# PSUM as three shared pairs of banks, and four tiles of scores in a row, in a graph attention kernel of 32 batches

## The chip, the cores and the metric

The kernel runs on one core of one Trainium2 chip. The metric is the device time of one execution in microseconds (us); the figure for a kernel is the median of its runs.

## What is computed

Two layers over 32 batches of 512 nodes with 512 features, all in float32. The first is masked attention with 8 heads of 64, the second a graph convolution; each is added to its input and normalized.

```python
# layer 0
q, k, v = (x @ Wq + bq), (x @ Wk + bk), (x @ Wv + bv)      # per head: 512 x 64
scores = einsum('bihd,bjhd->bhij', q, k) / sqrt(64) + where(adj == 0, -1e9, 0)
out = einsum('bhij,bjhd->bihd', softmax(scores), v)
x = layernorm(x + out)
# layer 1
deg_inv_sqrt = where(adj.sum(1) > 0, rsqrt(adj.sum(1)), 0)
norm_adj = adj * deg_inv_sqrt[:, None] * deg_inv_sqrt[None, :]
x = layernorm(x + norm_adj @ (x @ weight) + bias)
```

## The kernel before

**Steps.** The work is a list of 128 steps, `blocks`: one for each batch and each pair of heads (`ORDER`, four pairs). The loop over `k` (line 819) writes one step after another in program order; a wrapper, `InOrder`, keeps every engine in exactly this order, and every instruction therefore carries the wrapper's line, L44, in the profile. So groups are told apart by tile names.

**One step.** The scores of a step are four tiles, each 128 keys by two heads by 512 queries, two banks of PSUM each. `scores((b, g, jj))` makes two of them: TensorE writes `sc`, VectorE takes it out with the clip and the mask (`e<-sc,maskT`), ScalarE makes the exponential in place. `values` multiplies the exponentials of the step before with V into the one bank `av` (16 matmul instructions), and VectorE turns that bank (`yb<-av`). `accumulate` adds the four `e` tiles on GpSimd, one (`acc<-e`) and then two (`acc<-acc,e`) instructions, the last two put off through `pending` and `put_off`. `fold` turns and reduces that sum on VectorE one step later (`acc<-acc`, `folded<-acc`). In program order a step is: two tiles of scores, fold, values, two more tiles of scores, and then its share of other work.

**Shares.** The other work is what prepares the next batch and finishes the batch before. Each product with weights is done in a form with seven products of half size (`seven`, and `second` for the convolution); one product fills one bank (`mm`) with 8 matmul instructions and is then taken out by VectorE, at times by ScalarE. `cut` deals the products of a batch over its four steps. In the steady part (batches 2 to 30) the four kinds of step are called here:
- step a (line 821, `at == 1`): the seven products of V (`values_of`) and the first of K and Q, with the tail of the convolution's layer norm (`rest`: statistics, root, stores), the inverse of the softmax sums (`inverse_all`), `scale` (VectorE, `yT<-yT,inv`) and `add` (GpSimd, `yT<-yT,xr`);
- step b: the next eight products of K and Q (`keys_and_queries`), with the attention's layer norm: `measure` (VectorE), `root` (GpSimd, `rstd` and `add`), `norm` (ScalarE, `yT<-yT,add,rstd` and `hi<-yT,dis`), `low` (VectorE, `lo<-yT,dis,hi`), `lift` (GpSimd, `yT<-yT,b_r`);
- step c: products of K and Q, and the first half of the convolution (`first`, four products of twice the length in time, taken out by ScalarE);
- step d: the last product of K and Q and the seven of `second`, with the first two `measure` of the convolution's layer norm.

The dictionary `beside` (line 849) says behind which product each small piece stands. On GpSimd, in step a, the sum `u<-u,bv_r` stands between the fourth and the fifth product of V: VectorE waits for it.

**PSUM.** Eight banks: `ps_mm` has three single banks for products, `ps_sc` two pairs for scores, `ps_av` one bank.

The `e` tiles have six buffers: the third and fourth tile of a step are written over the first two of the step before, which `values` of this step reads.

Of the kernel before, what the change touches and what calls it, by code (L numbers as in the profile page):

```python
# [9 lines left out]
F32 = mybir.dt.float32  # L10
# [7 lines left out]
P = 128  # L18
H = 8
# [30 lines left out]
def unshifted(  # L50
# [37 lines left out]
    acts = ctx.enter_context(tc.tile_pool(name="acts", bufs=2))  # L88
    work = ctx.enter_context(tc.tile_pool(name="work", bufs=2))
    small = ctx.enter_context(tc.tile_pool(name="small", bufs=3))  # L90
    ps_mm = ctx.enter_context(tc.tile_pool(name="ps_mm", bufs=3, space=bass.MemoryType.PSUM))
    ps_sc = ctx.enter_context(tc.tile_pool(name="ps_sc", bufs=2, space=bass.MemoryType.PSUM))
    ps_av = ctx.enter_context(tc.tile_pool(name="ps_av", bufs=1, space=bass.MemoryType.PSUM))

# [28 lines left out]

    def turn_first(j, i):

        p = ps_mm.tile([P, 2, HALF], F32, name="mm")
        for n in range(2):
            for u in range(2):  # L130
                for q in range(4):
                    at = q * P + (2 * i + u) * 32
                    tensor.matmul(
                        p[32 * q : 32 * (q + 1), u, ts(n, P)], R[0][2 * j + n][:, at : at + 32], ident,
                        start=True, stop=True,
                    )
        (scalar.copy if i else vector.tensor_copy)(XT[:, 2 * j + i], p)
# [103 lines left out]
    def adjacency(m):  # L241


        p = ps_mm.tile([P, N], F32, name="mm")
        for n in range(NT):
            tensor.transpose(p[:, ts(n, P)], adj_sb[:, n, ts(m, P)], ident)
        vector.tensor_scalar(maskT[:, m, :], p, 0.0, FAR, op0=ALU.is_equal, op1=ALU.mult)
        scalar.copy(adjT[:, m, :], p)
        scalar.copy(plainT[:, m, :], p)
# [36 lines left out]
    def seven(multiply, first, middle, out):  # L286

        t = {}

        def piece(k, i, j):  # L290
            p = ps_mm.tile([P, 2, HALF], F32, name="mm")
            multiply(p, i, j)
            if k == 0:
                t["e1"] = work.tile([P, 2, HALF], F32, name="e1", bufs=1)
                first(t["e1"], p)
            elif k == 1:
                vector.tensor_add(out(0, 0), t["e1"], p)
            elif k == 2:
                t["u1"] = t["e1"]
                vector.tensor_add(t["u1"], t["e1"], p)  # L300
            elif k == 3:
                t["u2"] = work.tile([P, 2, HALF], F32, name="u2", bufs=1)
                middle(t["u2"], t["u1"], p)
            elif k == 4:
                vector.tensor_add(out(1, 1), t["u2"], p)
                vector.tensor_add(t["u1"], t["u1"], p)
            elif k == 5:
                vector.tensor_sub(out(1, 0), t["u2"], p)
            elif k == 6:
                vector.tensor_add(out(0, 1), t["u1"], p)  # L310

        order = [(0, 0), (1, 1), (5, 5), (6, 6), (4, 4), (3, 2), (2, 3)]
        return [(2.1, piece, (k, *args)) for k, args in enumerate(order)]
# [59 lines left out]
    def scores(s):  # L373

        b, g, jj = s
        E[s] = [work.tile([P, 2, N], F32, name="e", bufs=6) for _ in range(2)]
        for l in range(2):
            j = 2 * jj + l
            e = E[s][l]
            p = ps_sc.tile([P, 2, N], F32, name="sc")  # L380
            for k in range(2):
                r = slice(k * HD, (k + 1) * HD)
                tensor.matmul(p[:, k, :], KQ[b, g][r, 0, ts(j, P)], KQ[b, g][r, 1, :], start=True, stop=True)
            vector.scalar_tensor_tensor(
                e, p, CUT, maskT[:, j, None, :].to_broadcast([P, 2, N]), op0=ALU.min, op1=ALU.subtract
            )
            scalar.activation(e, e, AF.Exp)
# [20 lines left out]
    def values(s):  # L408

        b, g, jj = s  # L410
        e = E.pop(s)
        if jj == 0:
            AV[b, g] = ps_av.tile([P, N], F32, name="av")
        av = AV[b, g]
        for l in range(2):
            j = 2 * jj + l
            for k in range(2):
                tensor.matmul(
                    av[k * HD : (k + 1) * HD, :], V[b][:, j, ts(2 * g + k, HD)], e[l][:, k, :],
                    start=j == 0, stop=j == NT - 1,  # L420
                )
        if jj == 0:
            return
        if (b, g) == blocks[-1]:
            turned = work.tile([P, N], F32, name="avT", tag="yb", bufs=1)
            scalar.copy(turned[:, :HALF], av[:, :HALF])
            vector.tensor_copy(turned[:, HALF:], av[:, HALF:])
            AV[b, g] = turned
            return

        yb = work.tile([P, 4, NT, 32], F32, name="yb", bufs=1)
        vector.transpose(
            yb.rearrange("p l i s -> p i l s"), av.rearrange("p (i r l) -> p i l r", i=NT, l=4)
        )
        if g == ORDER[0]:
            if b < B - 1:
                YT[b] = acts.tile([P, NT, D], F32, name="yT")
            else:  # L440
                YT[b] = wv[:, :NT].rearrange("p k u o -> p k (u o)")
        for q in range(4):
            nc.sync.dma_start(
                YT[b][:, :, (4 * g + q) * 32 : (4 * g + q + 1) * 32],
                yb[32 * q : 32 * (q + 1)],
            )
# [13 lines left out]
    def sums(b, c):  # L460


        p = ps_mm.tile([P, N], F32, name="mm")
        for q in range(4):
            parts = ACC[b, ORDER[2 * c + q // 2]]
            for k, a in enumerate(parts):
# [31 lines left out]
    def finish(b):  # L498
# [3 lines left out]

        def inverse_all():

            p = ps_mm.tile([P, H, NT, 4], F32, name="mm")
            tensor.matmul(
                p.rearrange("p h i l -> p (h i l)"), spread.rearrange("p q r -> p (q r)"),
                SM[b].rearrange("p h t -> p (h t)"), start=True, stop=True,
# [8 lines left out]

        def inverse(cs):
            sT = SM[b]
            p = ps_mm.tile([P, NT, 2, 2, 32], F32, name="mm")  # L520
            for i in range(NT):
                tensor.transpose(p[:, i].rearrange("p a k r -> p (a k r)"), sT[:, ts(i, P)], ident)
            if cs[0] == 0:
# [22 lines left out]

        def turn_values(g):

            t["y"] = ps_mm.tile([P, NT, P], F32, name="mm")
            for i in range(NT):  # L550
                tensor.transpose(t["y"][:, i], AV[b, g][:, ts(i, P)], ident)

# [9 lines left out]
                )  # L562

        def measure(i):
            if i == 0:
                t["mv"] = small.tile([P, NT, 2], F32, name="mv")
            statistics(YT[b][:, i, :], t["mv"][:, i, :])

# [35 lines left out]
        def block(f):  # L604
            return [(0, f, (i,)) for i in range(NT)]

        return dict(
            early=[(0.6, inverse, ((0,),))], late=[(0.6, inverse, ((1,),)), (0.6, turn_values, (ORDER[-1],))],
            pairs=[[(0, add_pair, (i, g)) for i in range(NT)] for g in ORDER],
            halves=[(0, root, (0, 2)), (0, root, (2, 2))],  # L610
            inverse=[(0.6, inverse_all, ())], scale=block(scale), add=block(add), measure=block(measure), root=[(0, root, ())],
            judge=[(0, judge, ())], norm=block(norm), low=block(low), lift=block(lift), grow=block(grow),
        )

    def weave(side, main):
# [8 lines left out]
    def convolve(b):  # L624
# [3 lines left out]
        last = b == B - 1  # L628

        def first(d):  # L630
            p = ps_mm.tile([P, N], F32, name="mm")
            for m in range(NT):
                tensor.matmul(p, HI[b][:, m, ts(d, P)], adjT[:, m, :], start=m == 0, stop=False)
                tensor.matmul(p, LO[b][m][:, ts(d, P)], adjT[:, m, :], start=False, stop=m == NT - 1)
# [1 line left out]

        def block(m):
            if m == 0:
                t["p"] = [ps_sc.tile([P, 2, N], F32, name="sc") for _ in range(2)]
            for part, start, stop in ((HI[b][:, m, :], m == 0, False), (LO[b][m], False, m == NT - 1)):  # L640
                for d in range(DT):
                    p = t["p"][d // 2][:, d % 2]
# [23 lines left out]
            return tile[:, 2 * j : 2 * j + 2, ts(i, HALF)]  # L666

        def second(k, i, j):
            p = ps_mm.tile([P, 2, HALF], F32, name="mm")
            for r in range(2):  # L670
                for u in range(2):
                    tensor.matmul(
# [146 lines left out]
    for k in range(S + 1):  # L819
        b, at = divmod(k, G)  # L820
        if at == 1:
# [22 lines left out]
            elif b < B - 1:  # L844
# [2 lines left out]


                beside = {
                    0: rest[:1], 1: rest[1:3], 3: rest[3:4] + put_off, 4: rest[4:5],  # L850
                    5: rest[5:6] + f["inverse"] + put_off, 6: rest[6:] + f["scale"][:2], 7: f["scale"][2:] + f["add"],
                    8: measure[:2] + put_off, 9: measure[2:], 10: f["root"] + put_off, 11: norm[:1],
                    12: norm[1:2] + low[:1], 13: norm[2:3] + low[1:2], 14: norm[3:] + low[2:3],
                    15: low[3:] + f["lift"], 16: put_off + grow[:2], 17: put_off + grow[2:], 18: turn0 + f["judge"],
                }
                side = sum(([piece] + beside.get(i, []) for i, piece in enumerate(main)), [])
                side += c["first"] + c["parts"] + kq[5:] + turn1[:1]
# [33 lines left out]
            run(early[:2])  # L891
        if k and blocks[k - 1][0] < B - 1:
            fold(*blocks[k - 1])
        if k:
            values((*blocks[k - 1], 0))
            if k == S:
# [3 lines left out]
                sums(blocks[k - 1][0], (k - 1) % G // 2)  # L900
        if k == S - 2:
            run(within)
            scores((*blocks[k], 1))
            pending += [((*blocks[k], jj),) for jj in range(2)]
        elif k < S:
            accumulate((*blocks[k], 0))
            scores((*blocks[k], 1))
            if b == B - 1:
                accumulate((*blocks[k], 1))
            else:  # L910
# [29 lines left out]
    run(e["unload"] + e["parts"] + s[6:] + end["grow"] + extend[2:] + c["measure"][:2])  # L940
    s, tail, halves = e["second"], c["measure"][2:] + c["root"] + c["store"], e["halves"]
    run(s[:2] + halves[0] + s[2:3] + tail[:1] + s[3:4] + tail[1:3] + s[4:5])
    p = ps_mm.tile([1, 1], F32, name="mm")
    tensor.matmul(p, count, ones, start=True, stop=True)
    vector.tensor_scalar(bad, p, -1.0, float(P * B * NT * H + N), op0=ALU.mult, op1=ALU.add)
    run(tail[3:] + s[6:] + e["measure"][2:] + e["roots"][1:] + e["stores"][2:] + s[5:6] + halves[1] + e["roots"][:1])
# [284 lines left out]
```

## Time and profile before

| | |
|---|---|
| median of 3 runs | 2856.01 us (2855.47 to 2856.58) |
| the profiled execution, its own time | 2858.47 us |
| its span, first to last instruction | 2856.4 us |
| granted TensorE clock | 0.997 |
| TensorE weight loads, busy | 1865.2 us (65%) |
| VectorE, busy | 2301.6 us (81%) |
| GpSimd, busy | 1846.0 us (65%) |
| ScalarE, busy | 1046.8 us (37%) |
| DMA, mean | 49 GB/s |
| one batch in the steady part | 87.79 us (1312.35 to 1400.14) |

All times within the span are counted from its start. In the timeline a row reads: start, duration, engine, line, operation, out<-in, shapes, number of equal instructions that follow each other, and in brackets the idle time before it and what ended it. A float32 matmul of the program is two matmul instructions on the engine. "mean ns" of an instruction is its own latency; instructions of one engine overlap at their ends, so what a row costs is read from the start of the next.

### The profile page before, as it was taken

To read this page: it belongs to the slowest core of one execution; us is meant where nothing else is said; L and a number is where in the kernel's file an instruction comes from. 1 tells how busy PE (TensorE), PEld (TensorE's weight loads), DVE (VectorE), ACT (ScalarE), POOL (GpSimd) and SP (SyncE) were. 2 spreads that over 40 slices of the span, in tenths; PEclk is the share of its full clock that TensorE was granted. 3 is DMA by queue.
4 is the path that set the end of the run, shared out by engine and by line. 5 is a ranking of instruction groups with operands and counts; after the bars stand their busy time and mean duration, and the time that the engine had idled before them with its cause. 6 is when DMAs were issued, how large, how long until landed. Compare 5 with 4: busy or idle time off the path is not lost.

```text
span 2856.4 us, 34678 instructions
## 1 busy us (share of the span) xinstructions
PE 2817.5 (99%) x12540; PEld 1865.2 (65%) x12540; DVE 2301.6 (81%) x3201; ACT 1046.8 (37%) x1323; POOL 1846.0 (65%) x1174
## 2 busy tenths in 40 slices
PE   8999999999999999999999999999999999999997
PEld 6566666666666666666666666666666666666655
DVE  5878877888778887788887788877888778788787
ACT  2333333343333433333333334333343333333344
POOL 3666666766666666666666676666666666666666
PEclk9999999999999999999999999999999999999999
DMA  4111122111221112221112211122112222111211
GB/s 118 32 29 48 49 56 46 41 47 49 59 56 42 37 48 56 56 45 41 49 48 58 51 41 41 50 58 56 41 37 51 53 56 45 41 49 48 59 38 50
DMA packets 379108, 141.05 MB, mean 49 GB/s; under 512 B 277808, under 2 KB 345392, under 8 KB 378928
## 3 DMA queue, kind: packets, MB, share of 16 engines
q1 hardware_dynamic: 377776, 137.17, 20.1%
q8 instruction: 101, 1.65, 0.2%
q10 hardware_dynamic: 1152, 1.57, 0.2%
q14 instruction: 79, 0.65, 0.1%
HBM read 71.83 MB, written 33.55 MB: 37 GB/s over the span
## 4 chain that ended last, share of the span: by engine, by line
PE 78%; DVE 19%; issue 2%; POOL 0%; DMA 0%; ACT 0%; DVEq 0%; POOLq 0%; ACTq 0%
PE mm L44 52%; PE sc L44 13%; PE av L44 12%; DVE yT L44 5%; DVE e L44 5%; DVE st L44 3%; DVE acc L44 1%; DVE u L44 1%; DVE mv L44 1%; DVE yb L44 1%; DVE v L44 1%; DVE kq L44 1%; DVE xT L44 0%; DVE plainT L44 0%; POOL xT L44 0%
## 5 line engine op out<-in xcount | busy, mean ns | idle before, releaser
L44 ACT ACTIVATE e<-e 128x1024 f32<-128x1024 f32 x512 | 540.8, 1057 | 1166.2 <-DVE e L44 1137.2
L44 POOL TENSOR_TENSOR acc<-acc,e 128x1024 f32<-128x1024 f32 x248 | 588.9, 2375 | 188.3 <-ACT e L44 181.0
L44 DVE SCALAR_TENSOR_TENSOR e<-sc,maskT 128x1024 f32<-128x1024 f32 x512 | 597.5, 1207 | 22.1 <-PE sc L44 21.9
L44 PE MATMUL sc<-kq 64*128 64x512 f32 x2048 | 523.2, 623 | 3.5 <-DVE e L44 3.3
L44 PE MATMUL mm<-xT,wk 128*128 128x256 f32 x1792 | 476.3, 388 | 13.7 <-DVE u L44 11.3
L44 PE MATMUL av<-e,v 128*64 128x512 f32 x2048 | 467.9, 598 | 0.0
L44 PE MATMUL mm<-xT,wq 128*128 128x256 f32 x1792 | 460.7, 380 | 0.0
L44 POOL TENSOR_TENSOR acc<-e 128x1024 f32<-128x1024 f32 x126 | 297.2, 2358 | 230.4 <-ACT e L44 230.4
L44 PEld LDWEIGHTS mm<-xT,wk 128*128 128x128 f32 x1792 | 327.8, 190 | 143.1 <-issue 73.1
L44 PE MATMUL mm<-wv,xT 128*128 128x256 f32 x1792 | 404.3, 383 | 1.7 <-DVE xT L44 1.1
L44 PEld LDWEIGHTS mm<-wv,xT 128*128 128x128 f32 x1792 | 335.6, 190 | 72.3 <-issue 25.4
L44 PEld LDWEIGHTS mm<-xT,wq 128*128 128x128 f32 x1792 | 341.1, 190 | 46.5
L44 PEld LDWEIGHTS sc<-kq 64*128 64x128 f32 x2048 | 171.3, 186 | 290.7 <-issue 150.9
L44 PEld LDWEIGHTS av<-e,v 128*64 128x64 f32 x2048 | 135.5, 136 | 316.2 <-issue 293.4
L44 PE MATMUL mm<-w,zT 128*128 128x256 f32 x992 | 224.9, 379 | 0.7 <-ACT side L44 0.7
L44 POOL TENSOR_TENSOR rstd<-ve,minus_half 128x4 f32<-128x4 f32 (+1 forms) x66 | 66.2, 1003 | 232.5 <-DVE nmu L44 232.5
L44 DVE TENSOR_TENSOR kq<-u,mm 128x512 f32<-128x512 f32 x128 | 87.8, 686 | 156.5 <-PE mm L44 153.0
L44 POOL TENSOR_TENSOR yT<-yT,b_r 128x512 f32<-128x512 f32 x124 | 171.2, 1392 | 63.3 <-DVE lo L44 63.3
L44 PEld LDWEIGHTS mm<-w,zT 128*128 128x128 f32 x992 | 188.2, 190 | 28.1 <-issue 1.5
L44 POOL TENSOR_TENSOR yT<-yT,xr 128x512 f32<-128x512 f32 x124 | 192.8, 1584 | 18.8 <-DVE yT L44 18.8
L44 PE MATMUL mm<-adjT,hi 128*128 128x512 f32 x496 | 202.0, 407 | 0.0
L44 PE MATMUL mm<-adjT,lo 128*128 128x512 f32 x496 | 196.0, 395 | 0.9 <-DVE lo L44 0.9
(141 smaller groups left out, 3382.8 us busy)
## 6 DMA issues: line engine op xcount, KB each, us to landing
out_dram<-y SPq DMA_DIRECT2D x127, 256.0 KB, 2.1
x<-in_x_dram SPq DMA_DIRECT2D x248, 128.0 KB, 2.9
yT<-yb SPq DMA_DIRECT2D x496, 64.0 KB, 2.5
xr<-in_x_dram SPq DMA_DIRECT2D x122, 256.0 KB, 3.3
wk<-in_L_gnn_Wk_dram SPq DMA_DIRECT2D x8, 128.0 KB, 5.0
wq<-in_L_gnn_Wq_dram SPq DMA_DIRECT2D x8, 128.0 KB, 4.3
yT<-in_adj_dram SPq DMA_DIRECT2D x1, 1024.0 KB, 6.4
w<-in_L_gnn_weight_dram SPq DMA_DIRECT2D x2, 512.0 KB, 8.1
```

Of the source, the lines that this page charges most:

```text
L44: return self.tc.keep_in_program_order(op(*args, **kwargs))
```

## The change

Four things are edited in `unshifted`; the program has the same arithmetic, in another order.

1. One pool `psum` with three pairs of banks (`WIDE`), one single bank (`narrow`) and one for `av`. Scores always take pairs. A product takes what is next in the order pair, pair, pair, single (it uses one bank of a pair); the count starts anew in each step behind the scores.
2. Both calls of `scores` stand together, ahead of `values`. `fold` stands between them.
3. In `beside`, `root` of the attention's layer norm stands one product earlier and `norm` with it, `inverse` one product earlier and `scale` with it; the put-off sums of GpSimd stand behind the first two products of step a (before: behind the fourth and sixth).
4. `behind` puts block 3 ahead of blocks 0, 1, 2 in `add`, `measure`, `lift` and `grow`. `add` and `lift` are GpSimd's. Since `scale` and `low` on VectorE go in the order 0 to 3, GpSimd now begins when VectorE has done the last block; before, it began when VectorE had done the first.

```diff
-    ps_mm = ctx.enter_context(tc.tile_pool(name="ps_mm", bufs=3, space=bass.MemoryType.PSUM))
-    ps_sc = ctx.enter_context(tc.tile_pool(name="ps_sc", bufs=2, space=bass.MemoryType.PSUM))
-    ps_av = ctx.enter_context(tc.tile_pool(name="ps_av", bufs=1, space=bass.MemoryType.PSUM))
+    psum = ctx.enter_context(tc.tile_pool(name="psum", bufs=1, space=bass.MemoryType.PSUM))
+    WIDE = dict(tag="wide", bufs=3)
+    turn_of = {"n": 0, "order": (WIDE, WIDE, WIDE, dict(tag="narrow"))}
+
+    def bank(shape, tags=None):
+        if tags is None:
+            order = turn_of["order"]
+            tags = order[turn_of["n"] % len(order)]
+            turn_of["n"] += 1
+        return psum.tile(shape, F32, name="mm", **tags)
...
-            p = ps_sc.tile([P, 2, N], F32, name="sc")
+            p = psum.tile([P, 2, N], F32, name="sc", **WIDE)
...
+        def behind(f):
+            return [(0, f, (i,)) for i in (NT - 1, *range(NT - 1))]
...
-            inverse=[(0.6, inverse_all, ())], scale=block(scale), add=block(add), measure=block(measure), root=[(0, root, ())],
-            judge=[(0, judge, ())], norm=block(norm), low=block(low), lift=block(lift), grow=block(grow),
+            inverse=[(0.6, inverse_all, ())], scale=block(scale), add=behind(add),
+            measure=block(measure) if b == B - 1 else behind(measure), root=[(0, root, ())],
+            judge=[(0, judge, ())], norm=block(norm), low=block(low),
+            lift=block(lift) if b == B - 1 else behind(lift), grow=block(grow) if b == B - 1 else behind(grow),
...
-                    0: rest[:1], 1: rest[1:3], 3: rest[3:4] + put_off, 4: rest[4:5],
-                    5: rest[5:6] + f["inverse"] + put_off, 6: rest[6:] + f["scale"][:2], 7: f["scale"][2:] + f["add"],
-                    8: measure[:2] + put_off, 9: measure[2:], 10: f["root"] + put_off, 11: norm[:1],
-                    12: norm[1:2] + low[:1], 13: norm[2:3] + low[1:2], 14: norm[3:] + low[2:3],
-                    15: low[3:] + f["lift"], 16: put_off + grow[:2], 17: put_off + grow[2:], 18: turn0 + f["judge"],
+                    0: rest[:1] + put_off, 1: rest[1:3] + put_off, 3: rest[3:4], 4: rest[4:5] + f["inverse"],
+                    5: rest[5:6] + f["scale"][:2], 6: rest[6:] + f["scale"][2:] + f["add"],
+                    8: measure[:2] + put_off, 9: measure[2:] + f["root"] + put_off, 10: norm[:1], 11: norm[1:2],
+                    12: norm[2:3] + low[:1], 13: norm[3:] + low[1:2], 14: low[2:3], 15: low[3:] + f["lift"],
+                    16: put_off, 17: put_off + grow[:2], 18: grow[2:] + turn0 + f["judge"],
...
+        if k < S:
+            scores((*blocks[k], 1))
+        else:
+            turn_of["order"] = WIDE, dict(tag="narrow"), dict(tag="av")
+        turn_of["n"] = 0
         if k:
             values((*blocks[k - 1], 0))
...
         elif k < S:
             accumulate((*blocks[k], 0))
-            scores((*blocks[k], 1))
```

Every other `ps_mm.tile(...)` becomes `bank(...)`; `inverse_all` always takes the single bank, and the convolution's `block` of the last batch takes pairs.

## The prediction

> **What bounds the kernel now.** First the page, part 1:
>
> ```profile
> PE 2817.5 (99%) x12540; PEld 1865.2 (65%) x12540; DVE 2301.6 (81%) x3201; ACT 1046.8 (37%) x1323; POOL 1846.0 (65%) x1174
> ```
>
> TensorE is busy all through, and the wait list gives it only one repeated wait (below, 0.38 us in each batch). So the time is TensorE's own order of work plus small losses, and a batch repeats every 87.79 us. I therefore read where TensorE loses time without showing as idle. The timeline of TensorE alone, in one step d:
>
> ```profile
> 1341.96 3.65 PE L44 MATMUL av<-e,v 128*64 128x512 f32 x16
> 1345.55 1.99 PE L44 MATMUL sc<-kq 64*128 64x512 f32 x8
> 1347.47 1.13 PE L44 MATMUL mm<-xT,wk 128*128 128x256 f32 x4
> ...
> 1346.08 1.45 PE L44 MATMUL sc<-kq 64*128 64x512 f32 x6
> ...
> 1346.51 1.02 PE L44 MATMUL sc<-kq 64*128 64x512 f32 x4
> ```
>
> The last two rows are the same run of scores, entered later by a narrower window: its pairs of matmuls start at 1345.55, 1346.08, 1346.51, and the product follows at 1347.47. So pairs are 0.53, 0.43, 0.43, 0.53 apart: a run pays 0.10 on entering and 0.10 on leaving. Values take 3.59 with theirs.
>
> Next, how late VectorE takes up the first tile of a step (the lag D, from the start of the scores), TensorE's rows and then VectorE's, for steps c, a, b:
>
> ```profile
> 1317.72 1.99 PE L44 MATMUL sc<-kq 64*128 64x512 f32 x8
> 1323.30 2.26 PE L44 MATMUL sc<-kq 64*128 64x512 f32 x8
> ...
> 1361.48 1.99 PE L44 MATMUL sc<-kq 64*128 64x512 f32 x8
> ...
> 1383.24 1.99 PE L44 MATMUL sc<-kq 64*128 64x512 f32 x8
> ...
> 1400.14 1.13 PE L44 MATMUL mm<-xT,wk 128*128 128x256 f32 x4 [0.38 <-DVE u L44]
> ```
> ```profile
> 1322.03 2.34 DVE L44 SCALAR_TENSOR_TENSOR e<-sc,maskT 128x1024 f32<-128x1024 f32 x2
> ...
> 1363.61 2.32 DVE L44 SCALAR_TENSOR_TENSOR e<-sc,maskT 128x1024 f32<-128x1024 f32 x2
> ...
> 1382.22 5.18 DVE L44 TENSOR_TENSOR yT<-yT,inv 128x512 f32<-128x512 f32 x4
> 1387.33 2.34 DVE L44 SCALAR_TENSOR_TENSOR e<-sc,maskT 128x1024 f32<-128x1024 f32 x2
> ```
>
> D is 4.31 in c, 2.13 in a, 4.09 in b; in d it is 1.18, no lag (1341.22 against 1340.05). It costs almost nothing now, because between the first tile and the third, which takes the first one's banks, TensorE has 5.5 us of other work. In c the third tile does wait: it starts at 1323.30, 1.27 after VectorE began the first. This 1.27 is what a freed pair costs.
>
> [...] scores use 64 rows, values 64 columns, products the whole array, and each border shows about 0.10 twice. [...] four beside GpSimd's `yT<-yT,xr` took 5.18; two with GpSimd idle took 1.29 (0.60 apart):
>
> ```profile
> 2759.13 1.29 DVE L44 TENSOR_TENSOR yT<-yT,inv 128x512 f32<-128x512 f32 x2
> ```
>
> [...] That is the 0.38 wait: with three banks the fourth product in a row waits for `u`.
>
> **The change, part by part**, in one steady batch; times from the start of a step's scores.
>
> *Four tiles in a row.* One run of scores less per step: 0.20 (its two extras), so 4 x 0.20 = 0.80 gone. The first matmul behind the values pays on entering as it does now behind scores.
>
> *Four banks for products.* The wait for `u` goes: 0.54 (from 1399.60, where the product was due, to 1400.14), 0.10 for entering again, 0.08 of a smaller one before it: 0.72 in step b. In c the waits of the third and fourth tile (0.33), in b one of 0.10, go with the old order.
>
> *Three pairs for four tiles.* New: the fourth tile takes the first tile's pair. It is due at 0.10 + 6 x 0.43 = 2.68 and may start at D + 1.27; so a lag above 1.41 is paid in full, with 0.10 for entering again. Behind it stand values and all products of the step. Products then start 4.64 behind the fourth tile (0.96 for it, 0.09, 3.59), or at 7.22 without a wait; before, at 7.42.
>
> *Lag in a.* VectorE ends d with two sums of the last product, ready only when scores begin, and one statistics pair; nothing of this is edited. D stays 2.13: fourth tile at 3.40, products at 8.04.
>
> *Lag in b.* GpSimd's order in a becomes sum, sum, `rstd`, `add`, sum, `u<-u,bv_r`; before, `u` came ahead of the put-off sums. First product out at 10.07, two statistics, the second at 11.80, `ve` at 13.2; `rstd` and `add` 1.5 (1374.20 to 1375.74), so 14.7; sum 2.36, 17.05; `u` 1.27, 18.3. It would be done at 17.3 without that sum: 1.0 late. VectorE waits for it, then: two V instructions 1.2, inverse 1.25, one 0.6, two `scale`, one 0.6, two `scale`. By `behind`, GpSimd has nothing to do meanwhile, so four `scale` cost 2.4 and not 5.1. Sum 18.3 + 6.05 = 24.4. The step is 8.04 + 14.34 (1368.90 to 1383.24) = 22.38 long. D = 2.1 with a semaphore delay or two; fourth tile at 3.37, products at 8.01.
>
> *Lag in c.* In b: product out at 10.04, four statistics of 0.81 and two products of 0.60, 14.5; `rstd` and `add` to 16.0; ScalarE four times `norm` (0.84 + 0.63), 21.9; its two halves of `e<-mm,bias` stand behind these, 22.7; VectorE `kq` 0.6, last `low` 0.65 without GpSimd beside it, 24.0. Step b is 8.01 + 14.73 - 0.72 = 22.02. D = 1.95; fourth tile at 3.22, products at 7.86.
>
> *Lag in d.* Behind the convolution VectorE has one product: D = 1.18, no wait.
>
> Sum of the batch: a 22.38; b 22.02; c 7.86 + 14.57 = 22.43; d 7.22 + 14.01 = 21.23: 88.06, against 87.79. So +0.27 for each batch: 1.95 is saved, and three waits of 0.82, 0.79 and 0.64 take its place. Over 30 batches +8.
>
> *Both ends.* In the first batch nothing ahead of the lag is edited: by the same rule its D of 4.36, 2.13, 1.88 and, at 127.27, 7.59 cost 2.5, 0.6, 0.4 and 1.1, less 0.2 in one step: +4. At the end of the last batch D is 6.26 in one step (its products are few), worth about 4; behind it TensorE has waits of 1.07, 0.89 and 2.36 on slower chains, which take up part: bounds 0 to +4, I take +2.
>
> *Hidden edits.* The DMAs are the same in kind and number, SP's order too; DMA's mean is 49 GB/s. `lift` and `grow` come later by 2 to 3 us but are needed only in the next step (`lift` ends near 7 of c, `grow` near 13, the convolution's second half is a step away). Without that cover each late us would stand in d.
>
> Total: 2856.4 + 8 + 4 + 2 = 2870 of span. The profiled execution took 2858.5 with a span of 2856.4, the median of the runs is 2856.0; so I add 14 to the median: 2870.
>
> **Rivals.**
>
> Lag gone (faster): GpSimd's sum gets ahead of `rstd`, or ScalarE's chain is shorter than I add up, so that D in b and c falls under 1.41. Then b is 21.23 and c 21.79: 86.63 for a batch, -1.16, -35 in 30; with +4 at the ends 2825. For it: only 0.7 and 0.5 us decide. Against: each step of both chains has a measured row. It decides from D = 1.41 down, 0.1 of lag being worth 3 us in all per step kind.
>
> No relief (slower by much): GpSimd's blocks still meet VectorE's `scale` and `low`, because GpSimd ends step a late. Then D in b grows by 2.7, in c by up to 0.8: +3.5 x 30 = 105, 2975. Against: `add` waits for the last `scale` in the changed program's own waits.
>
> No difference: entering again after a wait costs nothing in a row of scores, -0.3 x 30 = -9 and the ends absorb theirs: 2858. Against: the third tile in c pays it today (1323.30 to the product at 1325.48 is 2.18, not 1.92).
>
> **How the numbers follow.** Likeliest 0.57, at 2870, its own range 2860 to 2884 (each D right to 0.2, so 6 us for each of two steps, and 0 to +4 at the end). Lag gone 0.22; no difference 0.13; no relief 0.08. A measurement of this kernel tells 0.2% (5.7 us) from no change. Slower 0.57 + 0.08 = 0.65, same 0.13, faster 0.22. The range reaches to 2832, inside the first rival, and to 2886; what is left out is the far part of it and the last.
>
> **What would show it.** Right: runs of 16 score matmuls with 3.6 for values behind them; a wait of the fourth tile on `e` of 0.6 to 0.8 in a, b, c and none in d; no wait on `u`; four `scale` in about 2.5 us. Wrong: fourth tiles without waits in b and c, a product that waits for a pair, or `scale` still at 1.3 each. It is wrong in its root if a batch does not take 88.0 to 88.2 us.

## The result, and the profile after

The changed kernel takes 2884.39 us (median of 4 runs, 2883.42 to 2884.67), the kernel before on the same chip 2856.3 us (2855.47 to 2857.94). The ratio is 1.0097, interval [1.0084, 1.0109]: slower by 28 us, where 14 were predicted. The profiled execution took 2884.41 us with a span of 2882.4, granted clock 0.996.

Where the time went is read from TensorE's timeline: the start of the first score matmul of a step cuts the span. Steps are numbered by the loop's `k`; the steady part is k = 6 to 123, 29.5 batches.

| part of the span | before | after | difference | predicted |
|---|---|---|---|---|
| up to the first scores | 55.24 | 51.95 | -3.3 | left out |
| k = 0 to 5 | 98.80 | 106.68 | +7.9 | +4 |
| k = 6 to 123 | 2590.79 | 2606.49 | +15.7 | +8 |
| k = 124 to 126 | 48.25 | 53.10 | +4.9 | +2, with the next row |
| k = 127 and the tail | 63.3 | 64.2 | +0.9 | |
| span | 2856.4 | 2882.4 | +26.0 | +14 |

The other 2 us of the 28 lie outside: before's profiled execution was 2.2 above the median of its runs, after's was not. The means of the steps a, b, c, d (b from k = 10 on: in after the first, k = 6, has a D of 1.25 and no wait):

| | a | b | c | d | batch |
|---|---|---|---|---|---|
| D before | 2.13 | 4.10 | 4.30 | 1.18 | |
| D after | 2.13 | 1.99 | 2.19 | 1.18 | |
| start of the fourth tile, after | 3.38 | 3.26 | 3.47 | 2.68 | |
| length before | 21.75 | 22.30 | 22.32 | 21.43 | 87.80 |
| length after | 22.55 | 21.91 | 22.67 | 21.23 | 88.37 |

TensorE's timeline of after, from the last products of a step d into the scores of a step c (in brackets the idle time before a row and what ended it):

```profile
1460.84 2.85 PE L44 MATMUL sc<-kq 64*128 64x512 f32 x12
1464.22 1.13 PE L44 MATMUL sc<-kq 64*128 64x512 f32 x4 [0.53 <-DVE e L44]
1465.28 3.65 PE L44 MATMUL av<-e,v 128*64 128x512 f32 x16
...
1477.82 3.62 PE L44 MATMUL mm<-wv,xT 128*128 128x256 f32 x16
1481.49 1.10 PE L44 MATMUL mm<-xT,wk 128*128 128x256 f32 x4
...
1483.39 2.85 PE L44 MATMUL sc<-kq 64*128 64x512 f32 x12
1486.65 1.13 PE L44 MATMUL sc<-kq 64*128 64x512 f32 x4 [0.42 <-DVE e L44]
...
1505.31 2.85 PE L44 MATMUL sc<-kq 64*128 64x512 f32 x12
1508.77 1.13 PE L44 MATMUL sc<-kq 64*128 64x512 f32 x4 [0.62 <-DVE e L44]
```

Three tiles run together, and the fourth waits for VectorE to take up the first: 0.53, 0.42 and 0.62 of idle time in a, b and c. From one start to the next the delay is larger, since the fourth tile is due 2.68 after the step's start: 0.70, 0.58, 0.78. The row that follows a wait is 0.10 longer from its start to the next (1464.22 to 1465.28 is 1.06; two pairs of score matmuls and a border are 0.96).

The same stretch on VectorE:

```profile
1462.97 2.32 DVE L44 SCALAR_TENSOR_TENSOR e<-sc,maskT 128x1024 f32<-128x1024 f32 x2
...
1476.07 0.69 DVE L44 TENSOR_TENSOR u<-e,mm 128x512 f32<-128x512 f32 x1 [1.04 <-PE mm L44]
1479.28 0.69 DVE L44 TENSOR_TENSOR v<-u,mm 128x512 f32<-128x512 f32 x1 [2.52 <-POOL u L44]
...
1480.48 0.87 DVE L44 TENSOR_SCALAR inv<-mm 32x32 f32<-32x32 f32 x4
...
1482.37 1.29 DVE L44 TENSOR_TENSOR yT<-yT,inv 128x512 f32<-128x512 f32 x2
...
1484.17 1.29 DVE L44 TENSOR_TENSOR yT<-yT,inv 128x512 f32<-128x512 f32 x2
1485.38 2.35 DVE L44 SCALAR_TENSOR_TENSOR e<-sc,maskT 128x1024 f32<-128x1024 f32 x2
```

The four `scale` (`yT<-yT,inv`) are at 1.29 for two, no longer 5.18 for four. Ahead of them VectorE stands 2.52 us for `u`. GpSimd shows why: its put-off sum stands ahead of `u`.

```profile
1475.50 0.20 POOL L44 TENSOR_TENSOR add<-nmu,rstd 128x4 f32<-128x4 f32 x1
1475.65 2.37 POOL L44 TENSOR_TENSOR acc<-acc,e 128x1024 f32<-128x1024 f32 x1
1477.98 1.27 POOL L44 TENSOR_TENSOR u<-u,bv_r 128x512 f32<-128x512 f32 x1
```

So the four `inv<-mm` on VectorE, which free the single bank of `inverse_all`, begin at 1480.48 and end at 1481.35; the first product of K and Q takes that bank. It starts at 1481.49, 0.22 later than it was due, and another 0.08 goes on entering again (the row is 0.94 long to the next start; unhindered it is 0.86). This is a product that waits for a bank, the kind of sign that the prediction listed under "wrong". And a batch takes 88.37, outside the 88.0 to 88.2 beyond which the prediction called itself wrong in its root; the experiments show how much of it stands.

### The profile page after: what moved, and what is told of

It is laid out like the page before. It is cut to its first block, busy times and chain, and to the rows that moved or that the text cites. A ratio compares the mean times of both kernels' runs of the same rounds, so it can differ in the third digit from the quotient of the medians.

```text
span 2882.4 us, 34572 instructions
## 1 busy us (share of the span) xinstructions
PE 2800.4 (97%) x12540; PEld 1873.0 (65%) x12540; DVE 2160.6 (75%) x3201; ACT 1052.6 (37%) x1323; POOL 1785.5 (62%) x1174
## 3 DMA queue, kind: packets, MB, share of 16 engines
q8 instruction: 101, 1.65, 0.2%
## 4 chain that ended last, share of the span: by engine, by line
PE 74%; DVE 18%; POOL 4%; issue 2%; ACT 1%; DMA 0%; POOLq 0%; SPq 0%; ACTq 0%; DVEq 0%
PE mm L44 50%; PE av L44 16%; PE sc L44 8%; DVE e L44 4%; DVE v L44 3%; DVE yT L44 3%; DVE st L44 2%; DVE y L44 2%; POOL u L44 1%; POOL acc L44 1%; DVE inv L44 1%; POOL rstd L44 1%; ACT e L44 1%; DVE lo L44 1%; DVE kq L44 1%
## 5 line engine op out<-in xcount | busy, mean ns | idle before, releaser
L44 PE MATMUL sc<-kq 64*128 64x512 f32 x2048 | 503.3, 615 | 58.2 <-DVE e L44 56.1
L44 PEld LDWEIGHTS sc<-kq 64*128 64x128 f32 x2048 | 179.2, 186 | 316.1 <-issue 148.8
L44 POOL TENSOR_TENSOR yT<-yT,b_r 128x512 f32<-128x512 f32 x124 | 154.5, 1279 | 193.3 <-DVE lo L44 193.3
L44 POOL TENSOR_TENSOR yT<-yT,xr 128x512 f32<-128x512 f32 x124 | 154.4, 1278 | 189.4 <-DVE yT L44 189.4
L44 POOL TENSOR_TENSOR parts<-zT 128x512 f32<-128x512 f32 x62 | 78.7, 1269 | 188.9 <-PE mm L44 188.9
```

What stands on the lines that cost most here:

```text
L44: return self.tc.keep_in_program_order(op(*args, **kwargs))
```

## The experiments

Ratios are to the kernel before, run beside each. Lengths of steps and D are read from each run's own trace, as in the tables above.

**Only the order of blocks, on the kernel before.** The edits of `behind` alone:

```diff
-            ... add=block(add), measure=block(measure), ... lift=block(lift), grow=block(grow),
+            ... add=behind(add), measure=block(measure) if b == B - 1 else behind(measure), ...
+            lift=block(lift) if b == B - 1 else behind(lift), grow=block(grow) if b == B - 1 else behind(grow),
```

> The kernel before, with only the order of add, measure, lift and grow changed (block 3 ahead of 0, 1, 2). Theory (the cost of the change sits in TensorE's wait for the first pair of scores; with two tiles ahead of the values there is no such wait, so VectorE's lag decides nothing): the four scale take about 2.5 us and not 5.2, D in step b falls from 4.1 to about 1.5, and the time stays within 4 us of 2856. Rival (the new order itself costs, because add, measure and lift begin later): slower by 10 us or more.

Measured: 2820.8 us, ratio 0.9874 [0.9859, 0.9889]. Both expectations missed. D in b fell to 1.94, as expected, but the batch went from 87.80 to 86.60: b from 22.30 to 21.43, c from 22.32 to 21.98. No wait for `u` is left. The stalls of before, which the prediction had put down to too few banks, go without another bank.

**Only `add`.** To see which of the four edits does it:

```diff
-            ... scale=block(scale), add=block(add),
+            ... scale=block(scale), add=behind(add),
```

> The kernel before, with only GpSimd's add begun with block 3 (measure, lift and grow as before). Theory (scale on VectorE is slow because add runs beside it; the wait for u in step b and its smaller ones follow from that): scale takes 2.5 us, D in step b is 1.9, step b takes 21.43 and not 22.30; lift still runs beside low, so step c keeps a D near 4 and at least half of its 0.34: 2825 to 2831 us. Rival (the gain of the order behind comes from lift and measure): 2845 us or more.

Measured: 2822.66 us, ratio 0.9879 [0.9863, 0.9894]; the batch is 86.60 again, b 21.43 and c 21.98. VectorE's timeline of this run, the end of a step a:

```profile
1366.15 3.04 DVE L44 TENSOR_TENSOR yT<-yT,inv 128x512 f32<-128x512 f32 x4
1369.11 2.34 DVE L44 SCALAR_TENSOR_TENSOR e<-sc,maskT 128x1024 f32<-128x1024 f32 x2
```

Four `scale` in 2.96, where they took 5.11 in before, and the scores are taken up that much earlier. In this run GpSimd begins `add` at 1369.27, behind the last `scale`; in before it ran beside three of the four (the prediction shows `scale` from 1382.22):

```profile
1383.53 6.24 POOL L44 TENSOR_TENSOR yT<-yT,xr 128x512 f32<-128x512 f32 x4 [0.63 <-DVE yT L44]
```

The wait for `u` in step b of before was VectorE's lateness, carried through the step. c's wait goes too, although D is still 3.06 there (`lift` beside `low`): with the old order of scores the third tile is due at 5.50 and may start at D + 1.27, so it waits only from D = 4.23 up; before had 4.30. The expectation that half of c's 0.34 stays was wrong for that reason.

**The old order of scores, on the changed kernel.**

```diff
         if k < S:
-            scores((*blocks[k], 1))
...
             accumulate((*blocks[k], 0))
+            scores((*blocks[k], 1))
...
+        if k < S:
+            turn_of["n"] = 0
```

> The changed kernel, with only the second pair of score tiles put back behind the values. Theory: the four runs of scores cost 0.20 each again (+0.80 a batch), the waits of the fourth tile go (0.70, 0.58 and 0.78 with 0.10 each for entering again: -2.36), the wait for the single bank in step a (0.29) stays; a batch takes about 86.9 us, and with shorter ends the time is 2829 us, faster than both kernels by 27 and 55. Rival 1 (the four banks for products bring nothing once the order is the old one, the wait for u only moves): 2856. Rival 2 (the loss lies in sharing pairs of banks between scores and products, not in the order): about 2884, as the changed kernel.

Measured: 2825.46 us, ratio 0.9890 [0.9875, 0.9905]; batch 86.79. The theory holds in size. But against the first experiment, with the same order of scores and banks of their own, nothing is gained in the steady part: the shared banks and the new places in `beside`, which this run has too, together cost 0.19, all in step a (21.95 against 21.76).

**The same, with `u` ahead of one sum.** In `beside`, as in the experiment after this one, with the old order of scores:

> The changed kernel with the second pair of score tiles behind the values and one put-off sum behind u: the order of before with the shared banks. Theory: the 0.19 by which step a was longer with shared banks (21.95 against 21.76) is the wait for the single bank; with u earlier it goes, step a takes 21.76 and the batch 86.60, as in the kernel before with the order behind alone: 2820 us. Rival (sharing the pairs costs step a something else): step a stays at 21.9 and the time at 2825.

Measured: 2818.45 us, ratio 0.9865 [0.9849, 0.9882]. Step a is 21.65 long: the 0.19 went and 0.10 more. So the 0.19 hangs on the sum ahead of `u`, behind which the product waits for the single bank. The batch is 86.49, 0.11 under the first experiment's; what of this is the shared banks' and what the other new places' was not tried apart.

**`u` ahead of one sum, on the changed kernel.**

```diff
-                    0: rest[:1] + put_off, 1: rest[1:3] + put_off, 3: rest[3:4], ...
+                    0: rest[:1] + put_off, 1: rest[1:3], 3: rest[3:4] + put_off, ...
```

> The changed kernel, with one of GpSimd's put-off sums in step a moved from behind the second to behind the fourth product, so behind u. Theory: u ends 1.3 us earlier, the wait of 0.22 for the single bank in step a goes with its 0.07 for entering again, D in step b falls from 1.99 to 1.2 at most and with it the wait of the fourth tile (0.58 and 0.10); D in step c stays, as its chain runs behind step b's own products. -0.97 a batch, 2856 us. Rival (a wait that goes comes back in the next step, since the chain of layer norm is as long as before): D in step c grows by 0.7 and the time falls by no more than 9 us.

Measured: 2852.15 us, ratio 0.9984 [0.9978, 0.9991]. a fell by 0.30, b by 0.68 to 21.23, with D at 1.18; c stays at 22.65. -1.00 a batch: the waits are additive here, and nothing came back in c.

**The lag of step a.**

```diff
-                    side += turn1[3:4] + s[5:6] + c["measure"][:1] + turn1[4:] + s[6:] + c["measure"][1:2]
-                    rest = c["measure"][2:] + c["root"] + c["store"]
+                    side += turn1[3:4] + s[5:6] + c["measure"][:1] + turn1[4:] + s[6:]
+                    rest = c["measure"][1:] + c["root"] + c["store"]
```

(the indices of `rest` in `beside` move by one)

> The changed kernel, with one statistics pair of the convolution's layer norm (0.87 us on VectorE) moved from the end of step d to behind the first product of step a. Theory: D in step a falls from 2.13 to about 1.3 and its wait (0.70 and 0.10) goes; but the pair now stands ahead of rstd, so u, which stands behind the put-off sum behind rstd, ends 0.85 later, and the wait for the single bank at the end of step a grows by as much: step a stays within 0.15 us of its length, the time within 5 us of 2884. Rival (each wait has its own price, 0.80 a batch here): 2860 us.

Measured: 2872.56 us, ratio 1.0055 [1.0041, 1.0069], between the two. D in a fell to 1.31 and its wait went. The wait for the single bank grew, but by less than the 0.85 expected, since VectorE makes up part of the pair: from taking out the first product of V to the start of `ve` it takes 3.73 where after took 3.27, 0.46 more for a pair of 0.87, as the pair fills a gap of 0.22 and rows follow each other more closely. TensorE's wait list has it in every batch now, 0.51 us each (line waited for: us in total, times, longest):

```profile
PE mm L44 <- DVE inv L44: 15.2, 30, 0.5
```

From start to start the first product of K and Q is 0.68 late and not 0.22. Step a is 22.21 long: 0.80 saved, 0.46 given back at its own end.

**The lag of step c.**

```diff
-                    12: norm[2:3] + low[:1], 13: norm[3:] + low[1:2], 14: low[2:3], 15: low[3:] + f["lift"],
-                    16: put_off, 17: put_off + grow[:2], 18: grow[2:] + turn0 + f["judge"],
+                    12: norm[2:3] + low[:1], 13: low[1:2], 14: norm[3:] + low[2:3],
+                    16: low[3:] + f["lift"], 17: put_off, 18: put_off + grow + turn0 + f["judge"],
```

> The changed kernel, with the lag of step c taken away: the last norm on ScalarE stands behind e<-mm,bias in step b, and the last low with the four lift goes from the end of step b to behind the first product of step c. Theory: D in step c falls from 2.19 to about 1.3, its fourth tile starts at 2.68 and not 3.46, 0.88 a batch less, and no other step changes: 2858 us. Rival (the late low and lift push grow and the convolution's first half, so that the wait appears within step c): step c stays at 22.6 and the time at 2880 or more.

Measured: 2856.18 us, ratio 0.9998 [0.9990, 1.0006]. D in c is 1.18, its length 21.78, 0.89 less; the other steps are as they were.

**All three together.**

> The edits of the three lags together (a put-off sum behind u, the statistics pair of step d moved to step a, the last norm, low and lift moved back), on the changed kernel. Theory: steps without a wait are 21.56, 21.23, 21.78 and 21.23 long, 85.80 a batch, 0.80 under the kernel before with the order behind alone, as four runs of scores less are worth; the ends stay as in the changed kernel (106 and 53 us): 2809 us. Rival (four tiles in a row cost something besides these waits): a batch stays over 86.6 and the time over 2825.

Measured: 2804.11 us, ratio 0.9818 [0.9804, 0.9831]; 21.46, 21.23, 21.78 and 21.23, a batch of 85.70. TensorE's timeline of this run, a step b:

```profile
1444.42 3.70 PE L44 MATMUL sc<-kq 64*128 64x512 f32 x16
1448.06 3.65 PE L44 MATMUL av<-e,v 128*64 128x512 f32 x16
1451.64 1.13 PE L44 MATMUL mm<-xT,wk 128*128 128x256 f32 x4
```

Sixteen score matmuls stand in one row, and the products start 7.22 after it. Four tiles in a row are worth the 0.80 that the prediction gave them, once D is under 1.41 everywhere.

**The ends.** On the kernel of the three edits, the second pair of tiles goes behind the values where `k in (1, 5) or b == B - 1`.

> The kernel of the three lag edits, with the second pair of score tiles put back behind the values in three places alone: steps 1 and 5 and the last batch. Theory: the first batch falls from 106 to about 100 and the last from 53 to 48: 2798 us, faster than every other version. Rival (the ends are long because of the shared banks, not of the order): 2806 or more.

Measured: 2794.01 us, ratio 0.9779 [0.9766, 0.9793]: the fastest version, 63 us under the kernel before in the same runs and 90 under the changed one. k = 0 to 5 take 101.48 (106.67 without this edit), k = 124 to 126 take 48.01 (52.90).

**`add` begun with block 0, on the changed kernel.**

```diff
-            ... add=behind(add),
+            ... add=block(add),
```

> The changed kernel, with add begun with block 0 again, so that GpSimd's add runs beside VectorE's scale. Theory: the four scale take 2.6 us longer, D in step b grows from 1.99 to about 4.6 and the fourth tile's start from 3.26 to 5.9, all of it paid, +2.6 a batch: 2961 us. Rival 1 (as in the kernel before, where undoing this cost only 1.2 a batch): 2920 us. Rival 2 (add no longer meets scale, since the chain is earlier): 2884 us.

Measured: 2958.56 us, ratio 1.0358 [1.0340, 1.0375], batch 90.96. The size is as expected, but by luck, as its make-up is not. D in b grew by 1.55 only, to 3.54. VectorE's timeline:

```profile
1516.46 1.29 DVE L44 TENSOR_TENSOR yT<-yT,inv 128x512 f32<-128x512 f32 x2
...
1518.26 2.83 DVE L44 TENSOR_TENSOR yT<-yT,inv 128x512 f32<-128x512 f32 x2
1521.02 2.34 DVE L44 SCALAR_TENSOR_TENSOR e<-sc,maskT 128x1024 f32<-128x1024 f32 x2
```

GpSimd begins `add` at 1517.22, so two `scale` keep 1.29 and only the other two meet it. The rest of the loss is TensorE itself. Its timeline in two steps b of this run, with the same wait:

```profile
1432.40 1.13 PE L44 MATMUL sc<-kq 64*128 64x512 f32 x4 [1.96 <-DVE e L44]
1433.46 3.65 PE L44 MATMUL av<-e,v 128*64 128x512 f32 x16
```
```profile
1522.28 1.56 PE L44 MATMUL sc<-kq 64*128 64x512 f32 x4 [1.96 <-DVE e L44]
1523.77 4.87 PE L44 MATMUL av<-e,v 128*64 128x512 f32 x16
```

and around them, in stretches of 3.41 us, the granted clock (window; its length, TensorE's busy time and matmuls, granted clock, DMA share and GB/s):

```profile
1430.69:1434.10 3.41, 1.70 (x8) 1.00 0.00 0
1434.10:1437.52 3.42, 3.42 (x18) 1.00 0.00 0
```
```profile
1519.44:1522.85 3.41, 1.45 (x10) 1.00 0.00 0
1522.85:1526.26 3.41, 3.41 (x10) 0.50 0.00 0
```

After the second wait the matmuls run at a granted clock of 0.50 for 3.41 us: 0.43 more for the fourth tile and 1.22 more for the values, 1.65 in all. It happened in 18 of the 29 steps b from k = 10 to 122, always behind the same wait: these steps are 25.10 to 25.16 long, the other 11 are 23.46.

The half-clock stretches in these steps are 3.41 us long and start whole multiples of 3.41 apart (341.83, 522.74 and 614.90: 53 and 27 of them). Counted in intervals of 3.41 from these starts, the 29 waits differ: in all 18 slow steps at least 1.85 us of the wait lay in one interval, and the next interval ran at half clock; in the 11 others it was divided, with at most 1.79 in one.

## Why the prediction was half right

The direction, and the mechanism that it named as the likeliest, hold: lags that cost nothing between two pairs of tiles are paid in full by a fourth tile in a row. Taking any one of the three lags away takes its wait away. What failed is the size of two terms of the sum, +14 in all where +28 was measured. The steady batch was priced at +0.27 and costs +0.57: the late `u` was followed to step b's lag but not to the single bank in a, and step c's lag was taken 0.24 too short. The two ends were priced at +4 and +2 and cost +7.9 and +5.7: what the granted clock of 0.50 costs behind waits of 2.1 us and more was put at nothing (3.2 us more than before in the first batch, 1.6 in the last), and one lag of the last batch was left out. One more term had the right sum from a wrong cause, which is luck. By the prediction's own steps:

- **Four tiles in a row: right.** -0.80 a batch. With four in a row and no lag the batch is 85.70, with the old order and `u` ahead 86.49; step d, which never waits, is 21.23 with the one order and 21.43 with the other in every run.
- **The fourth tile may start at D + 1.27, due at 2.68: right.** At D of 1.99, 2.13 and 2.19 it started at 3.26, 3.38 and 3.47; at 1.18 and at 1.31 (the experiment on step a) it started at 2.68. The 0.10 on entering again is there each time. (The 0.26 that the prediction read from step c of before holds two such entries and a short wait of the fourth tile, which starts 1.13 behind the third and not 0.96.)
- **Four banks for products, 0.72 and 0.33 and 0.10: the sum right, the cause wrong.** Starting `add` last gives 1.20 a batch with the old banks. The wait for `u` was read as a shortage of banks because it is a product that waits; it was VectorE that came late, since `scale` had run beside `add` (D = 4.10). The prediction had both facts and used the second only for D. That the sum came out is luck. The shared banks with the changed places gave nothing in a steady batch: 0.19 more, or 0.11 less with `u` ahead. What speaks for them is the stretch up to the first scores: 50.9 to 52.5 in the nine traces with shared banks, 53.9 to 56.0 in the three without; that gain of some 3 us was left out of the sum.
- **Lag in a, wait 0.82: measured 0.80. But the length of a was under-sized:** 22.38 predicted, 22.55 measured. The prediction computed that `u` comes 1.0 late and followed this to D in b, not to the single bank, which the next product takes. That wait is 0.30 with its re-entry, as the experiment with `u` ahead shows (22.55 to 22.25).
- **Lag in b, 0.79: measured 0.68** (D 1.99, not 2.1).
- **Lag in c, 0.64: measured 0.89** (D 2.19, not 1.95). The chain was the right one: ScalarE's `e<-mm,bias` behind the last `norm`, then `kq`, `low` and the scores. VectorE's timeline of after has its end: `kq` waits 1.44 for ScalarE, and scores that began at 1505.31 are taken up at 1507.50.

```profile
1506.23 0.69 DVE L44 TENSOR_TENSOR kq<-e,mm 128x512 f32<-128x512 f32 x1 [1.44 <-ACT e L44]
1506.84 0.75 DVE L44 SCALAR_TENSOR_TENSOR lo<-yT,dis,hi 128x512 fp32r<-128x512 f32 x1
1507.50 2.35 DVE L44 SCALAR_TENSOR_TENSOR e<-sc,maskT 128x1024 f32<-128x1024 f32 x2
```

- **The batch, +0.27: measured +0.57.** (Its parts as the prediction lists them, 2.25 of waits less 1.95, give 0.30.) By the experiments: -1.20 for `add`, +0.19 for the shared banks with the new places in `beside`, -0.80 for the order of scores, and +2.37 for its three waits (0.80, 0.68, 0.89). This term, twice its forecast, is 8 of the 14 us that were missed: +15.7 in the steady part and not +8.
- **First batch, +4: measured +7.9.** The rule prices the waits, not what TensorE does after a long one. TensorE's timeline of after, k = 1:

```profile
65.48 1.99 PE L44 MATMUL sc<-kq 64*128 64x512 f32 x8
70.06 2.97 PE L44 MATMUL sc<-kq 64*128 64x512 f32 x8 [2.59 <-DVE e L44]
72.96 4.50 PE L44 MATMUL av<-e,v 128*64 128x512 f32 x16
```

  Behind 2.59 of waiting, eight score matmuls take 2.97 and not 1.99, the values 4.50 and not 3.65: 1.8 more; before has no such stretch in this step. In k = 5 before has one too (eight score matmuls take 3.68 behind a wait of 3.26, 1.7 more); in after it is longer, behind 4.02 of waiting: 2.08 in place of 1.13 for four and 5.75 in place of 3.65 for the values, 3.0 more. The granted clock of after was 0.50 from 71.3 to 74.7 and from 136.2 to 143.0, that of before from 136.2 to 139.6. So the slow matmuls explain 1.8 + 1.4 = 3.2 of the +7.9, most of what was missed; the waits make the other 4.7, near the +4. Part of these is another thing: the row that waits 2.59 in k = 1 begins with the third tile, not the fourth, and starts just after VectorE has taken out a product (`e<-e,mm`, 69.23 to 69.91). With the old order and shared banks k = 1 is long too, 16.27 where before has 14.93: its third tile is on time, but a product waits 1.48 for the scores.
- **Last batch, +2 within 0 to +4: measured +5.7.** The slack behind it took up nothing. The old order there gives 4.9 back. The prediction priced one lag, in k = 126; in k = 125, where D was 3.64, it named none, and there the fourth tile now waits 1.48 and the step is 1.55 longer. In k = 126 the third tile waits 2.10 and the fourth 0.45, and the granted clock behind them is 0.50 from 2798.6 to 2802.0: 2.08 for the fourth tile and 4.34 for the values, 1.6 more.
- **No relief, 2975, the rival with `scale` beside `add`:** not what happened. The part of it that was tried, `add` begun with block 0, took 2958.6, 74 over the changed kernel; the prediction's 105 has c's lag in it as well, which was not tried. Its 2.7 a batch for `scale` is near the 2.6 measured, but by luck: it was worked out from a lag alone, and two fifths of the cost was the clock (18 of 29 times 1.65, 1.0 of the 2.6 a batch).

## What to carry to other kernels

A stall is priced where it starts, not where it shows: ask of a product that waits for a bank whether the engine that empties the bank is late for a reason of its own, and try that cure by itself before rearranging memory. Before tiles that share buffers are put in one row, measure how late the consumer takes up the first; each step whose lag exceeds the run ahead of the reuse pays the excess, and such waits add up one by one, so they can also be removed one by one. Where a wait on TensorE reaches about two microseconds, add what the rows behind it may lose: here 1.65 us behind a wait of 1.96, in 18 of 29 steps.

## What the runs showed of the hardware

TensorE's granted clock was 0.50 for 3.41 us behind a wait of 1.96 in 18 of 29 steps b of the kernel with `add` begun with block 0; the other 11, with the same wait, are 1.64 to 1.70 shorter. The two groups differ in how the intervals of 3.41 divide the wait: at least 1.85 us of it in one in the 18, at most 1.79 in the 11. That is of these 29 waits; what work stands around the wait was not varied. In the changed kernel the clock was 0.50 for 3.4 us after 2.59 of waiting (k = 1), and for 6.8 from the last 0.5 of a wait of 4.02 on (k = 5). Behind the waits of 0.4 to 0.6 in its steady part it stayed at 1.00, and its steps of one kind differ there by 0.03 us at most. The loss was 1.65 us behind 1.96, and about 3.0 behind 4.02.

Two `scale` took 2.83 us beside GpSimd's `add` and 1.29 without it, 1.5 more in one row, and it adds up: beginning `add` with block 3 or block 0 moved the kernel before by 34 us and the changed one by 74, the clock included.
